# A convolution, spectral attention and FFN on one core: the main stage ordered by a table of places, 128-column weights in the last product, first pixels loaded ahead of the build

## The chip, the cores and the metric

One core of a Trainium2 chip runs the whole program in one launch. The metric is the device time of that launch in microseconds; each kernel is timed several times and the median counts. One further execution is recorded by the hardware profiler: all views of "the profile" and "the trace" come from it. PE is the matrix engine, PEld its weight loads, DVE, ACT and POOL are the vector, scalar and GpSimd engines, and SP only issues DMAs here.

## The reference, cut to what matters

The input x is 64 images of 55 x 55 pixels with 96 channels in float32. A depthwise convolution comes first, with a 25 x 25 kernel of which only every third row and column is non-zero and the centre is zero. Its result multiplies x. Then follow a spectral layer and a feed-forward layer, both residual and both on a layer norm over the channels, with each image taken as a sequence of 3025 tokens:

```python
x = conv(x, kernel * mask) * x + bias + x
t = x.reshape(64, 3025, 96)
h = relu(bn1(ln(t) @ w1.T))                      # 192 channels
X = fft(h, axis=1, norm='ortho')
xr = relu(X.real * rd - X.imag * idg + rb)
xi = relu(X.imag * rd + X.real * idg + ib)
t = t + bn2(ifft(xr + 1j * xi).real @ w2.T)
h = relu(qlinear(ln(t), W1, b1))                 # 384 channels, products in an 8-bit float
t = t + qlinear(h, W2, b2)
```

`qlinear` rounds its factors to a float with 5 exponent and 2 mantissa bits, and its sums to one with 10 mantissa bits (float16).

## The kernel before

**Build.** The convolution runs on PE with banded matrices made from the 81 taps. `sel` (selection matrices) and `kt` (taps) are loaded on SP's queue (L86 to L91), the network's constants on ACT's. For each of 56 PSUM banks, up to 20 small matmuls (L205) make a stretch of the bands; ACT copies the first 48 channels into `toep` (L214) and DVE the last 48 into `later` (L215), one 8.4 MB tile, which is then stored to DRAM as `tb` in six parts (L217). With that, the pools of the build are closed, and the output buffers of the convolution, `buf` (pool `c_ob`, six of them, L222), take their place in SBUF.

**Convolution.** The pixels of a third of the rows (r of 3), for half the images (bh of 2) and half the channels, form a group; there are 12. A group has four or three tiles of rows (`NTS`) and six steps of eight channels. `load` (L229) brings the x of a step, on SP's queue and always two steps ahead; the first two are asked for after `tb`'s stores (L304). `compute` (L237) takes two or three taps of tiles into a PSUM bank (L253), DVE adds 1 and multiplies by x into `buf` (L261), and POOL adds the bias (L271). `stores` (L275) gives the DMAs of a tile to the DRAM tensor `t1`, large ones on ACT's queue, small ones on POOL's. They are spread over the next group's steps, except that tiles whose buffer the next group needs at once are stored "early", right after their computing (L310 to L315). In the last group all three tiles are early, so their stores stand between the computing of one tile and the next. After the first six groups `toep` is refilled from `tb` (L317).

**Main stage.** Each of 64 sequences is a list of 289 tasks: load of t (L546), statistics (L560) and layer norm a (variance L508, root, reciprocal, Newton step L529), then seven times scale `xa`, turn `pa` (L587), copy `tnt`, and 13 times `ph` (L609), relu `h` (L618), transform `pf` (L624), copy `g` (L628), store to `gd`. Then come fetches `gt`; six spectral blocks (`px` L692, three ACT, four DVE and two POOL operations); four projections (`pd` L767, L777, `d` L786, `pe` L797, `e` L806); `ed` out and in; five inverse transforms `py` (L859) with residual and statistics; layer norm c; seven `xc`, `xq`, `pq` (L913), `tq`; nine times `pu` (L936), DVE's `y` (L945) and `z` (L948), ACT's `hq` (L960); five times `pw` (L981, "down": 15 matmuls, the weights of each being 121 columns of `hq`), ACT's and DVE's `o` (L990, L995), POOL's `ot` (L1001), store.

Every task has a place, a number in units of a sequence, which a formula gives, such as `at = fo + 0.231 + 1.552 * (...)[q]` at L1009. `ordered` (L371) goes through all tasks of all sequences with a model of each engine's time: for each engine, among the tasks that are free to run, it takes the one that can start soonest, but doesn't look past the first one that can start within 0.2 us by more than `NEAR` in place (0.359). The resulting order is written out as the program. Buffers (`bufs`, L464) come from pools with so many of each; PSUM has four small banks (`psn`) and two double ones (`psw`).

Of the kernel before, what the change touches and what calls it, by code (L numbers as in the profile page):

```python
# [11 lines left out]
F32 = mybir.dt.float32  # L12
# [29 lines left out]
NOB = 6  # L42
SU = 21
# [8 lines left out]

@with_exitstack
def conv_attn_hybrid(ctx, tc, a, out, t1, tb, gds, eds):
# [21 lines left out]
    with ExitStack() as cx:  # L76
# [9 lines left out]
        later = lp.tile([128, CHH, NE * TQ], F32, tag="later", name="later")  # L86
# [47 lines left out]
        for of in (toep, later):  # L134
            nc.gpsimd.memset(of[:, :, : 2 * TQ], 0.0)
            nc.gpsimd.memset(of[:, :, 16 * TQ :], 0.0)
# [61 lines left out]
        for j0 in range(0, TQ, 5):  # L198
            nj = min(5, TQ - j0)
            for e in range(2, 16):  # L200
# [14 lines left out]
                nc.vector.tensor_copy(later[:, :, cols], src[:, CHH:])  # L215
        for c0 in range(0, CHH, CC):
            nc.sync.dma_start(tb[:, c0 : c0 + CC], later[:, c0 : c0 + CC])  # L217
        first.close()

        ob = cx.enter_context(tc.tile_pool(name="c_ob", bufs=NOB))  # L222
        groups = [(0, r, bh) for r, bh in ((0, 0), (1, 0), (0, 1), (1, 1), (2, 0), (2, 1))]
        halfway = groups[-1]
        groups += [(1, r, bh) for bh in range(BH) for r in range(NR)]
        steps = [(n, c0) for n in range(len(groups)) for c0 in range(0, CHH, CC)]
        xts, bufs_ = {}, {}

        def load(n, c0):  # L229
            half, r, bh = groups[n]  # L230
            c1 = half * CHH + c0
            for m in range(NTS[r]):
                x = xp.tile([128, CC, NBS], F32, tag=f"x{m}", name=f"x{m}_{n}_{c0}")
                nc.sync.dma_start(x, a["xc"][bh, sum(NTS[:r]) + m][:, c1 : c1 + CC, :])
                xts[n, c0, m] = x
# [39 lines left out]
        def stores(n, m):  # L275

            half, r, bh = groups[n]
            rows_, buf, b0 = TPS[r], bufs_.pop((n, m)), bh * BB
# [3 lines left out]
            for i in range(nr):  # L282
                n0 = (3 * (rows_ * m + i) + r) * R
                large.append((
                    nc.sync if last and i % 2 else nc.scalar,
                    t1[b0 : b0 + BB, half, n0 : n0 + 48, :].rearrange("b (q s) c -> q b (s c)", s=3),
                    buf[at_row(i) : at_row(i) + 16].rearrange("q (b s) c -> q b (s c)", s=3),
                ))


            to = t1[b0 : b0 + BB, half].rearrange("b (y z) c -> y b (z c)", z=R)
# [12 lines left out]
        for step in steps[:2]:  # L304
            load(*step)
        for k, (n, c0) in enumerate(steps):
# [4 lines left out]
            for m in range(nt):  # L311
                compute(n, c0, m)
                if m < early:
# [6 lines left out]
            if ending:  # L320
                pending = [x for m in range(max(0, early), nt) for x in stores(n, m)]
# [21 lines left out]

    pools = {}
# [15 lines left out]
    tasks, users, edges = [], {}, {}  # L360
    FULL, SWITCH, NEAR, RING = "128x128", 0.09, 0.359, 8
    PLAIN = (FULL, FULL, 0.05, 0.05)

    def task(eng, cost, place, what, after=(), new=(), use=()):
        k = len(tasks)
        tasks.append((eng, cost, place, what, tuple(after), tuple(new), tuple(use) + tuple(h for h, _ in new)))
# [4 lines left out]
    def ordered(bufs):  # L371
# [11 lines left out]
        dma_free, last, landed = 0.0, PLAIN, []  # L383
# [22 lines left out]
        while len(order) < n:  # L406
            best = None
            for eng, q in queue.items():
# [3 lines left out]
                for place, k in q[:60]:  # L412
                    if first is not None and first[0] <= f + 0.2 and place > first[2] + NEAR:
                        break
                    r = max(f, ready_at[k])
                    wanted = [pool for _, pool in tasks[k][5]]
# [33 lines left out]
            else:  # L450
                free[eng] = end[k] = start + cost
            for h, pool in tasks[k][5]:
# [13 lines left out]
        e2=1, xc=2, xq=2, tq=1, hq=1, y16=2, z16=2, o16=2, ot=3, rstda=2, rstdc=2, mean=2, psn=4, psw=2,  # L466
# [4 lines left out]
    def make(h, pool, shape, dt=F32):  # L471
        k = count[pool] = count.get(pool, -1) + 1
        if pool == "tnt":
            live[h] = tnts[k % 2]
        elif pool in ("sm", "sr"):
# [23 lines left out]
    def layernorm_tasks(b, place, what, t, after, mean):  # L499

        st, rstd = (f"st{what}", b), (f"rstd{what}", b)
# [31 lines left out]

        new = [(mean, "mean")] if mean is not None else []
        k = task("POOL", 1.9 if new else 1.45, place + 0.048, variance, after, new=new, use=[st])
        k = task("ACT", 0.57, place, root, [k])
        k = task("DVE", 0.22, place, inverse, [k], new=[(rstd, f"rstd{what}")])
        return task("POOL", 1.12, place, newton, [k], use=[(rstd)])

    def sequence(b):  # L540
# [4 lines left out]
        def load():  # L545
            tt = make(t, "t", [NJ, 2, NR1, CHH])  # L546
            tv = t1[b].rearrange("h (j r) c -> j h r c", r=NR1)
# [3 lines left out]
        loaded = task("SP", (2, 0.41, 4.25), b - 0.85, load, new=[(t, "t")])  # L551
        sta = ("sta", b)
        ks = []
        for q in range(5):
# [9 lines left out]
            ks.append(task("DVE", 0.8, b - 0.6 - 0.214 + 0.06 * q, stats, after, new=new, use=[t] if new else [t, sta]))  # L564
        rstd = layernorm_tasks(b, b - 0.28, "a", t, ks, None)
        g_done = []
        for i in range(7):
            g0, ng = 4 * i, min(4, NR1 - 4 * i)
            at = b + 0.861 * (2 * i - 2.0) / 13
# [24 lines left out]
            k = task("POOL", 0.784 if ng == 4 else 0.31, at - 0.129, scale, [rstd], new=[(xa, "xa")], use=[t, ("rstda", b)])  # L594
            k = task("PE", 0.103 * ng, at, turn, [k], new=[(pt, "psn"), (tnt, "tnt")] + ([(gd, "gd")] if i == 0 else []), use=[xa])
            edges[k] = (FULL, FULL, 0.06, 0.1)
            turned_ = task("ACT", 0.1 + 0.087 * ng, at, turned, [k], use=[pt, tnt])
            ks = []
            for p in range(2 * i, min(2 * i + 2, 13)):
                nq = min(2, NR1 - 2 * p)  # L600
                at = b + 0.861 * p / 13
# [30 lines left out]
                k = task("PE", 0.326 * nq, at, hidden, [turned_], new=[(ph, "psn"), (h, "h")], use=[tnt])  # L632
                edges[k] = (FULL, FULL, 0.16, 0.16)
                k = task("ACT", 0.107 + 0.137 * nq, at, relu, [k], use=[ph, h])
# [510 lines left out]
```

## Time and profile before

| | us |
|---|---|
| median of 3 runs (lowest, highest) | 4614.85 (4613.04, 4620.83) |
| the profiled execution, and its span | 4654.67, 4652.9 |
| constants | 0 to 16 |
| build, PE busy throughout | 16.0 to 61.4 |
| PE idle: `tb` out, first x in | 62 to 86.5 |
| convolution, PE busy 789.5 of 863.9 | 86.5 to 950.4 |
| PE idle: handover | 950.4 to 1021.7 |
| main stage to the last `pf`, PE busy 3341.0 of 3496.3 | 1021.7 to 4518.0 |
| end, PE busy 102.4 of 134.9 | 4518.0 to 4652.9 |

The profiled execution is 0.9% longer than the median, and what is summed from its durations is compared with its own time first. Busy times of PE are modelled at their ends; where the pace of a row of matmuls matters, it is read from the starts in the timeline.

### The profile page before, as it was taken

To read this page: it belongs to the slowest core of one execution; us is meant where nothing else is said; L and a number is where in the kernel's file an instruction comes from. 1 tells how busy PE (TensorE), PEld (TensorE's weight loads), DVE (VectorE), ACT (ScalarE), POOL (GpSimd) and SP (SyncE) were. 2 spreads that over 40 slices of the span, in tenths; PEclk is the share of its full clock that TensorE was granted. 3 is DMA by queue.
4 is the path that set the end of the run, shared out by engine and by line. 5 is a ranking of instruction groups with operands and counts; after the bars stand their busy time and mean duration, and the time that the engine had idled before them with its cause. 6 is when DMAs were issued, how large, how long until landed. Compare 5 with 4: busy or idle time off the path is not lost.

```text
span 4652.9 us, 194788 instructions
## 1 busy us (share of the span) xinstructions
PE 4284.9 (92%) x83314; PEld 3569.2 (77%) x83314; DVE 3280.7 (71%) x7232; ACT 2963.2 (64%) x5947; POOL 3087.5 (66%) x4209
## 2 busy tenths in 40 slices
PE   7998798939999999999999999999999999999987
PEld 6998798937777777777777777777777777777775
DVE  4544354424888877877887788788787878788776
ACT  2000000017888888887887888888887888788875
POOL 1766576745666767766776666677766666677655
PEclk8999899969999999999999999999999999999996
DMA  4678888786666666766676666676666666667662
GB/s 162 166 193 204 245 197 207 190 185 165 165 171 178 179 177 178 181 177 169 180 183 169 169 174 179 172 185 180 176 183 169 177 174 176 171 179 183 177 162 71
DMA packets 572798, 823.14 MB, mean 177 GB/s; under 512 B 62127, under 2 KB 470276, under 8 KB 570268
## 3 DMA queue, kind: packets, MB, share of 16 engines
q1 hardware_dynamic: 442704, 736.10, 58.7%
q10 hardware_dynamic: 113036, 64.71, 7.1%
q0 software_dynamic: 16192, 9.86, 1.1%
q8 instruction: 655, 10.73, 1.0%
q14 instruction: 211, 1.73, 0.1%
HBM read 419.45 MB, written 390.64 MB: 174 GB/s over the span
## 4 chain that ended last, share of the span: by engine, by line
PE 71%; DVE 7%; DMA 7%; ACT 6%; issue 5%; POOL 2%; ACTq 2%; SPq 0%; POOLq 0%; DVEq 0%
PE pl L253 13%; PE pf L624 9%; PE ph L609 9%; PE pd L767 7%; PE px L692 7%; PE pw L981 5%; PE py L859 4%; PE pd L777 4%; PE pu L936 4%; PE pe L797 3%; PE pa L587 3%; DMA x<-in_xc_dram 2%; DMA t<-buf 2%; DVE y L945 2%; PE pq L913 2%
## 5 line engine op out<-in xcount | busy, mean ns | idle before, releaser
L253 PE MATMUL pl<-x,toep 128*64 128x96 f32 (+1 forms) x18432 | 790.1, 250 | 99.0 <-DVE buf L261 41.2
L253 PEld LDWEIGHTS pl<-x,toep 128*64 128x64 f32 (+1 forms) x18432 | 783.4, 137 | 105.7 <-issue 55.7
L945 DVE CAST y<-pu 128x1008 f16<-128x1008 f32 (+1 forms) x576 | 689.2, 1202 | 224.6 <-PE pu L936 220.5
L261 DVE SCALAR_TENSOR_TENSOR buf<-pl,x 121x384 f32<-121x384 f32 (+1 forms) x480 | 390.1, 842 | 499.0 <-PE pl L253 314.3
L609 PEld LDWEIGHTS ph<-w1e,tnt 97*121 97x121 f32 x3200 | 543.3, 185 | 210.9 <-issue 64.4
L960 ACT ACTIVATE hq<-z 128x1008 fp8e5<-128x1008 f16 (+1 forms) x576 | 601.2, 1050 | 156.7 <-DVE z L948 156.3
L718 DVE SCALAR_TENSOR_TENSOR m<-px,par,m 128x400 f32<-128x400 f32 x768 | 480.8, 626 | 286.3 <-ACT ar L709 201.6
L609 PE MATMUL ph<-w1e,tnt 97*121 97x192 f32 x3200 | 665.1, 330 | 12.9 <-ACT e L806 11.4
L271 POOL TENSOR_TENSOR buf<-buf,cbias 121x768 f32<-121x768 f32 (+1 forms) x240 | 434.1, 1821 | 363.9 <-DVE buf L261 252.1
L624 PE MATMUL pf<-h,f 121*128 121x384 f32 (+1 forms) x1664 | 664.8, 484 | 4.9 <-ACT h L618 2.6
L521 ACT ACTIVATE sm_s_a<-sm_v_a,eps 121x25 f32<-121x25 f32 x64 | 20.3, 318 | 959.0 <-POOL sm_v_a L512 956.6
L574 POOL TENSOR_TENSOR xa<-t,rstda 121x384 f32<-121x384 f32 (+1 forms) x448 | 348.2, 780 | 419.7 <-PE pa L587 411.7
L692 PE MATMUL px<-m,gt 50*64 50x50 f32 x24576 | 456.4, 220 | 63.1 <-issue 59.8
L692 PEld LDWEIGHTS px<-m,gt 50*64 50x64 f32 x24576 | 416.0, 136 | 122.0 <-issue 105.2
L725 POOL TENSOR_TENSOR sm<-ar,m 128x400 f32<-128x400 f32 x256 | 270.9, 1058 | 353.6 <-DVE m L718 296.4
L767 PE MATMUL pd<-w2e,sm 128*64 128x96 f32 x8192 | 415.7, 254 | 30.9 <-ACT g L628 18.0
L628 ACT COPY g<-pf 128x384 f32<-128x384 f32 (+1 forms) x832 | 385.6, 467 | 85.5 <-PE pf L624 70.6
L1001 POOL TENSOR_TENSOR ot<-t,o 121x480 f32<-121x480 f32 x320 | 374.3, 1177 | 91.2 <-DVE o L995 91.2
L618 ACT ACTIVATE h<-ph 121x384 f32<-121x384 f32 (+1 forms) x832 | 389.8, 488 | 68.3 <-PE ph L609 61.6
L948 DVE TENSOR_SCALAR z<-y,b1q 128x1008 f16<-128x1008 f16 (+1 forms) x576 | 418.9, 732 | 11.4
L767 PEld LDWEIGHTS pd<-w2e,sm 128*64 128x64 f32 x8192 | 358.6, 139 | 76.0 <-ACT g L628 22.5
L981 PEld LDWEIGHTS <-hq 128*121 128x121 fp8e5 x4800 | 315.9, 142 | 77.1 <-issue 37.6
(115 smaller groups left out, 8367.2 us busy)
## 6 DMA issues: line engine op xcount, KB each, us to landing
gd<-g SPq DMA_DIRECT2D x768, 192.0 KB
gt<-gd SPq DMA_DIRECT2D x512, 288.0 KB
x<-in_xc_dram SPq DMA_DIRECT2D x240, 384.0 KB
t<-t SPq DMA_DIRECT2D x64, 1050.0 KB
out_dram<-ot SPq DMA_DIRECT2D x320, 210.0 KB
t<-buf ACTq DMA_DIRECT2D x211, 288.0 KB
ed<-e SPq DMA_DIRECT2D x384, 150.0 KB
ed<-e SPq DMA_DIRECT2D x128, 131.2 KB
```

Source lines behind the costliest of these rows:

```text
L253: nc.tensor.matmul(pl[p : p + width, cc * NBS : (cc + 1) * NBS], toep[:, c0 + g + cc, o : o + width], xts[n, c0, m + d][:, g + cc, :], sta ...
L261: nc.vector.scalar_tensor_tensor(buf[:px, :, c0 + g : c0 + g + CG].rearrange("p n c -> p c n"), pl[:px, : CG * NBS].rearrange("p (c n) -> ...
L271: nc.gpsimd.tensor_tensor(part, part, cbias[:px, c1 : c1 + CC].unsqueeze(1).to_broadcast([px, NBS, CC]), ALU.add)
L609: nc.tensor.matmul(x[:NJ, q * H : (q + 1) * H], live[tnt][:, g * NJ : (g + 1) * NJ], w1e, start=True, stop=True,)
L624: nc.tensor.matmul(x[:, : nq * H], f1, live[h][:, : nq * H], start=True, stop=True)
L692: nc.tensor.matmul(x[to : to + 64].rearrange("p (q r n) -> p q r n", q=2, r=2)[:, k2p, :, o : o + NR1], y[rows, k % KC, c0 : c0 + 64], m1[ ...
L718: nc.vector.scalar_tensor_tensor(live[out_], view(px)[:, :, 256 : 256 + KC * NR1], scale, live[than], ALU.mult, ALU.max)
L767: nc.tensor.matmul(y[k % 2][64 * k2p : 64 * k2p + 64, k // 2 * CH : (k // 2 + 1) * CH], full[:, k, 64 * k2p : 64 * k2p + 64], w2e[:, 0, :] ...
L945: nc.vector.tensor_copy(live[y16][:, :n], live[pu][:, :n])
L948: nc.vector.tensor_scalar(make(z16, "z16", [128, 1024], F16)[:, :n], live[y16][:, :n], b1q[:, k : k + 1], 0.0, ALU.add, ALU.max,)
L960: nc.scalar.activation(live[hq][:, k, n0 : n0 + n], live[z16][:, :n], AF.Copy, saturate=False)
L981: nc.tensor.matmul(p[:NJ, g * CH : (g + 1) * CH], live[hq][:, k, n0 : n0 + NJ], w2q[:, k, :], start=(k == 0), stop=(k == 2),)
```

## The change

1. *Places.* A table of 289 numbers, one for each task of a sequence in the order in which they are defined, replaces the formulas: task k of the program gets `k // 289 + PLACES[k % 289]`. `NEAR` goes from 0.359 to 0.5.
2. *The model in `ordered`.* DVE's two bias tasks (`z`, L948, and `o`, L995) are put into `alone`: in the model they don't run at the same time as anything on POOL. A pool `small` of two stands for the small tiles of the layer norms. The cost given to `down` is 0.66 instead of 0.84, that to the bias of `o` 0.33 instead of 0.6.
3. *down.* `hq` becomes one fixed tile `hidden8` with seven zero columns at its end, in the pool `late`, and each weight of `pw` has 128 columns (of which the last seven give PSUM rows that nothing reads).
4. *Start.* The x of the first two steps are loaded first of all on SP's queue. The order of the groups' (r, bh) in the first half changes, so that the first group has three tiles. `later` becomes three tiles of 16 channels, with three copies for each bank.
5. *Handover.* In the last group the stores follow all the computing. `t1` becomes two DRAM tiles, one for each half of the images. The loads of sequences 0 and 1 are one DMA each, on POOL's queue.

```diff
+CPL = 16
+PLACES = (
+    -2.368, -0.491, -1.741, -2.267, -1.88, -4.257, -1.46, -0.301, -1.857, -0.171, -0.314, -0.137, -0.467,
...
+)
-        later = lp.tile([128, CHH, NE * TQ], F32, tag="later", name="later")
+        later = [lp.tile([128, CPL, NE * TQ], F32, tag=f"later{k}", name=f"later{k}") for k in range(CHH // CPL)]
+        groups = [(0, r, bh) for r, bh in ((1, 0), (0, 0), (1, 1), (0, 1), (2, 0), (2, 1))]
...
+        for step in steps[:2]:
+            load(*step)
         kt = selp.tile([128, CH], F32, tag="kt", name="kt")
         nc.sync.dma_start(kt, a["taps"])
...
                 nc.scalar.copy(toep[:, :, cols], src[:, :CHH])
-                nc.vector.tensor_copy(later[:, :, cols], src[:, CHH:])
+                for k, of in enumerate(later):
+                    c1 = CHH + CPL * k
+                    nc.vector.tensor_copy(of[:, :, cols], src[:, c1 : c1 + CPL])
         for c0 in range(0, CHH, CC):
-            nc.sync.dma_start(tb[:, c0 : c0 + CC], later[:, c0 : c0 + CC])
+            k, c1 = c0 // CPL, c0 % CPL
+            nc.sync.dma_start(tb[:, c0 : c0 + CC], later[k][:, c1 : c1 + CC])
...
-        groups = [(0, r, bh) for r, bh in ((0, 0), (1, 0), (0, 1), (1, 1), (2, 0), (2, 1))]
...
-                if m < early:
+                if m < early and n + 1 < len(groups):
...
-                pending = [x for m in range(max(0, early), nt) for x in stores(n, m)]
+                pending = [x for m in range(nt) if (n, m) in bufs_ for x in stores(n, m)]
...
+    hidden8 = late.tile([128, 3, NJ * NR1 + 7], F8, tag="hidden8", name="hidden8")
+    nc.gpsimd.memset(hidden8[:, :, NJ * NR1 :], 0.0)
...
-    FULL, SWITCH, NEAR, RING = "128x128", 0.09, 0.359, 8
+    FULL, SWITCH, NEAR, RING = "128x128", 0.09, 0.5, 8
...
-    def task(eng, cost, place, what, after=(), new=(), use=()):
+    def task(eng, cost, what, after=(), new=(), use=()):
         k = len(tasks)
+        place = k // len(PLACES) + PLACES[k % len(PLACES)]
...
                     r = max(f, ready_at[k])
+                    if eng == "POOL":
+                        r = max(r, shared)
+                    elif k in alone:
+                        r = max(r, free["POOL"])
...
                 free[eng] = end[k] = start + cost
+                if k in alone:
+                    shared = end[k]
...
-            tv = t1[b].rearrange("h (j r) c -> j h r c", r=NR1)
+            tv = t1s[b // BB][b % BB].rearrange("h (j r) c -> j h r c", r=NR1)
+            if b < 2:
+
+                nc.gpsimd.dma_start(tt, tv)
+                return
             for p0, p1 in split(NJ):
                 nc.sync.dma_start(tt[p0:p1], tv[p0:p1])
...
-                            p[:NJ, g * CH : (g + 1) * CH],
-                            live[hq][:, k, n0 : n0 + NJ],
+                            p[:, g * CH : (g + 1) * CH],
+                            live[hq][:, k, n0 : n0 + 128],
                             w2q[:, k, :],
...
-            k = task("PE", 0.84, at, down, [hq_done[s, k] for s in range((1, 2, 2, 3, 3)[q]) for k in range(3)], new=[(pw, "psn"), (o16, "o16")], use=[hq])
+            k = task("PE", 0.66, down, [hq_done[s, k] for s in range((1, 2, 2, 3, 3)[q]) for k in range(3)], new=[(pw, "psn"), (o16, "o16")], use=[hq])
```

In the program that results, the same tasks are issued on every engine, in another order.

## The prediction

> **What bounds the kernel now.** I read the page's head and 40 slices first, then the chain of waits at both ends of the convolution, then a table of windows, and last PE's waits and timeline in the steady part.
>
> From the page, its totals and PE's slices:
> ```profile
> span 4652.9 us, 194788 instructions
> PE 4284.9 (92%) x83314; PEld 3569.2 (77%) x83314; DVE 3280.7 (71%) x7232; ACT 2963.2 (64%) x5947; POOL 3087.5 (66%) x4209
> ...
> PE   7998798939999999999999999999999999999987
> q8 instruction: 655, 10.73, 1.0%
> ```
> PE is the bound wherever its digit is 9. It is less in the first slice, inside the convolution (slices 4 to 7), at the handover (the single 3, slice 9) and at the end. Windows (from:to and length; busy PE, PEld, DVE, ACT, POOL; granted clock, DMA share, GB/s) of two such places and of the steady main stage:
> ```profile
> 62.00:86.50 24.50, 0.58 (x4) 0.30 (x4) 0.11 (x1) 0.00 (x0) 0.00 (x0) 0.59 0.97 387
> 1400.00:4400.00 3000.00, 2873.43 (x53815) 2290.36 (x53813) 2411.38 (x5611) 2475.43 (x4968) 2102.78 (x3132) 0.99 0.68 177
> ```
> In the steady 3000 us, 2700 matmuls of ph at 50 a sequence make 54 sequences: 55.55 us each, of which PE is idle 2.34. All else in that stage is PE's own pace, and ACT at 82.5% comes next. The chain at the start and at the handover, in time order (start, length, piece):
> ```profile
> 16.02 45.35 PE pt L205 x1064
> ...
> 69.18 17.25 DMA x<-in_xc_dram
> ...
> 977.76 12.12 DMA t<-buf
> 989.96 13.86 DMA t<-t
> ...
> 1009.45 10.08 issue
> ...
> 1021.70 1.85 PE pa L587 x8
> ```
> After the build PE is idle 25 us while the stores of tb fill the DMA engines (0.97) and the first pixels land behind them. At the handover it is idle from 950.4 to 1021.7: last stores, first load of t, statistics, and 10.08 us in which sequence 0's reciprocal stands on DVE behind the statistics of sequence 1. In the steady part PE's waits (engine and line, releaser, total, times, longest) lead with:
> ```profile
> PE px L692 <- issue: 48.4, 50, 2.3
> PE pd L767 <- ACT g L628: 16.6, 27, 0.8
> ...
> PE ph L609 <- ACT e L806: 10.6, 27, 0.4
> ```
> About 82 of the 126.6 idle us are "issue", the rest waits for engines. The "issue" holes sit in long runs of small matmuls (px, pd, pe): two on the timeline, 2553.88 and 2558.45, are 4.57 us and 256 instructions (128 matmuls, 128 weight loads) apart; queue q8's 10.73 MB in 655 packets are 16.4 KB each. So I read them as PE reaching the next 256 instructions before they have been fetched.
>
> **What the Trainium skill says.** "TensorE: Matmul & The Clock Gate", section "Weight-path perf modes — Fast Weight Load (FWL) and DoubleRow": a weight load is fast, about twofold, when the number of weights is 128 and the type isn't FP32. The trace agrees; loads of min/median/max ns:
> ```profile
> L936 PEld LDWEIGHTS <-w1q x1152: 95/98/181, 1145.6 to 4637.1; 96*128 96x128 fp8e5 x192
> L981 PEld LDWEIGHTS <-hq x4800: 129/137/230, 1157.7 to 4646.3; 128*121 128x121 fp8e5 x192
> ```
> "SBUF — State Buffer", section "Who interferes with whom": a DVE operation in a two-port mode, or one with two SBUF inputs against a GpSimd read, takes the shared port alone and the other stands. L948 (372/597/1405 ns) and L995 (343/550/1308) spread as that says. "DMA: Bandwidth & Descriptors", section "Why a DMA increments its semaphore by 16 and not by 1": a transfer is dealt to the largest number of engines up to 16 that divides its rows, so 121 rows would get 11; no trace here shows it.
>
> **The change, part by part,** against the profiled run (4654.67, span 4652.9); the median shown, 4614.85, is 0.9% lower, so I scale at the end.
>
> *Start.* The first two steps' x (6 x 393 KB) now go ahead of kt and sel on SP's queue: 2.36 MB, about 6 us at the 387 GB/s above. The build starts at 16.02 behind the constants' chain (sc, w1e, pm), not behind sel, so this hides; sel's last part would land near 17. Three copies per bank on DVE instead of one (240 elements, by the trace's 240-element copies near 0.38 us each) stay below the 0.81 us that PE takes per bank (45.35/56). Then the convolution's matmuls can begin near 62.5, but DVE's first eviction writes buf, which lies over `later`, and so waits for all six stores of tb, until about 85. Eight PSUM banks hold only 4 of 2 taps at 1.32 us and 2 of 3 taps at 1.98, then 2 at 1.32 more: 11.9 us of PE work. So the gain is 12, not the 24 that the gap suggests. The other group order makes one more early store and costs nothing that I see.
>
> *Handover.* The last group's stores now follow all its computing, so POOL's last bias additions are no longer behind store issues: a few us earlier. t1 in two tiles frees nothing new: by region the loads of the first 32 sequences never waited for the other half's stores. Against the gain, hidden8 moves the pool of t upward until it reaches over the conv buffers, and the first loads of t_0 and t_2 now wait for the last stores on every DMA lane; then t_0 and t_1 (one DMA each on POOL's queue, of 121 rows), t_2 to t_4 (SP) and m1, m2 (ACT) all start together. Behind the waiting loads stand, on POOL, only work that needs t_0, and on SP t_3 and t_4, which aren't used for 100 us. The reciprocal is still queued on DVE behind t_1's statistics. I get 69 to 75 us against 71.3: 0, with 8 to 10 either way.
>
> *down with 128 columns.* On the timeline 15 matmuls of pw take 0.83 us (2576.16 to 2576.99), 55 ns each. Here 96 rows move (the 7 new columns are cleared once, on an idle POOL); pq moves 121 in 54 ns, so 96 should take 43 to 44. With loads of the 98 ns kind hidden, 15 x 44 = 0.66. 320 x 0.17 = **-54 us** of PE. Bounds: 0 (if pw's pace isn't the load's) and -60. Idle cover isn't in question: PE is the bound.
>
> *The order.* What the two programs issue on PE can be counted. Changes between full-array and 64-wide tiles: 716 before, 950 after. A ph followed by px lasts 0.74 us on the timeline instead of 0.65, so 0.09 each: 234 x 0.09 = +21. Short tasks (pa, pq, pw) directly ahead of ph or pf: 258 before, 384 after, at 0.01 (after pa) to 0.06 (after pq): +5, up to 8. PE's work is thus -54 + 21 + 5 = **-28**.
>
> *Fetch.* Runs of at least 128 small matmuls fall from 62 to 2, yet the densest 8 us hold as many instructions (640), and the densest 12 us hold 892 instead of 764. With one block of 256 instructions every 4.0 us and one block in hand, before's order loses 108 us over the main stage, near the 82 x 64/54 = 97 of the trace; after's loses 139 by the same sum. Bounds 0 and +31, I take **+15**: breaking the long runs should help more than my simple sum allows.
>
> *Engine waits.* 40 us in 54 sequences are 47 in 64, with start and end about 58. Slack, in PE work placed between producer and consumer, moves both ways: sm to pd at the 10th percentile 18.0 to 23.3 us, sr to pd2 11.3 to 18.1, hq to pw 2.3 to 4.6; but ph to pf has a median of 2.74 before and 1.30 after (10th percentile 1.72 and 0.81), pa to ph 2.87 and 1.30. A relu takes 0.49 (L618, mean 488 ns), and with both handoffs some 0.75 must fit. The waits on g and e (16.6 and 10.6) are for PSUM or buffers that ACT frees late; DVE is eased since z and o no longer run beside POOL (to near their minima, about 4 us a sequence). I take **-20**, between -58 and a growth that is priced as a rival.
>
> *End.* After the last pf, PE's pace of what is left is 67.4 us before and 61.7 after (its share of down included, already counted); 132 us pass in the trace, so most of the end is waiting on chains, which a shorter list improves a little: **-8**, 0 to -20.
>
> Sum: -12 + 0 - 28 + 15 - 20 - 8 = -53. 4614.85 x (1 - 53/4654.67) = **4562**.
>
> **The rivals.**
> *R1, a larger gain.* DVE's relief lets nearly all engine waits go (-58 for -20) and fetch holes stay as they are (0 for +15): -53 - 38 - 15 = -106, so 4510. For it: longer slack at every join of the spectral part. Against: ph to pf at half its former distance.
> *R2, slower.* One mechanism: ph to pf is placed at half its former distance, and ACT, at 82.5%, is late by more than the slack. The place is pf L624 <- ACT h, over 832 pf. It decides from 53/832 = 0.064 us per pf, where it undoes the forecast; I price it at 0.11, +92 less 53 = +39: **4653**. For it: a 10th percentile of 0.81 against 0.75 needed. Against: in the trace pf waited for h only 2.0 us in 54 sequences, and PE's queue delays itself, so one late relu makes the next one early.
> *R3, fetch takes it.* The densest stretches stall by the full +31, waits unchanged and the switches at 0.11 (+5), no gain at the end: -12 - 28 + 31 + 5 = -4, so 4611, no change to be told.
> *R4, the ends don't change as said.* The early pixels only move the wait to x of the third step or to the evictions (0 for -12), and the loads of t wait for the last stores (+10): -31, so 4584.
>
> **How the numbers follow.** Forecast 0.50, R1 0.15, R2 0.15, R3 0.10, R4 0.10. The likeliest is 4562, its own range 4535 to 4590 (waits, fetch and handover at half their bounds). For 8 in 10 the range takes in R1 (to 4505), R3 and R4, and cuts into R2: 4505 to 4640. A measurement of this kernel tells 0.2% (9 us) from no change: faster is the forecast, R1, R4 and a little of R3, 0.77; same 0.07; slower 0.16.
>
> **What would show it.** Loads of L981 near 98 ns and 15 pw in 0.66 to 0.67; PE idle from about 75 to 86 instead of 62 to 86; a gap at the handover of 62 to 80; L948 and L995 with medians near 400 and 360; PE busy in a steady 54 sequences lower by 20 to 30 us; px and pd "issue" near 90 to 115 us. Wrong if pf waits on h for over 50 us (R2), if "issue" doubles, or if pw keeps its 0.83.

## The result and the profile after

The changed kernel takes 4843.51 us (median of 4, 4833.11 to 4855.8) against 4617.84 for the kernel before, a ratio of 1.0489 (95% interval 1.0458 to 1.052). The prediction had 4562 and a range that ended at 4640. The profiled execution of the changed kernel took 4833.11 us.

| stage, us from the span's start | before | after |
|---|---|---|
| first matmul of the convolution | 85.6 | 60.3 |
| last matmul of the convolution | 950.4 | 919.0 |
| first `pa` of the main stage | 1021.7 | 1008.5 |
| main stage up to the last `pf`, length | 3496.7 | 3687.4 |
| end, length | 134.5 | 135.4 |

All of the loss, 190.7 us in these two profiles, lies in the main stage (in a second profile of each kernel it is 259.8 us, from 3484.9 to 3744.7). The two ends of the convolution together gave 13 us, which is what the sum had for them, though by other parts. From the page of the changed kernel, its head, PE's slices and the granted clock:

```profile
span 4831.3 us, 194630 instructions
PE 4327.9 (90%) x83314; PEld 3517.7 (73%) x83314; DVE 3215.5 (67%) x7344; ACT 2987.3 (62%) x5947; POOL 3085.4 (64%) x4216
...
PE   8999898569899998998999999999999999999996
...
PEclk9999999879999999999999999999999999999996
```

PE does the same 83,314 matmuls, those of `down` faster than before, and yet is busy 43 us longer. In the steady window (busy PE, PEld, DVE, ACT, POOL; clock, DMA share, GB/s):

```profile
1400.00:4400.00 3000.00, 2762.03 (x50927) 2135.55 (x50926) 2221.67 (x5310) 2362.10 (x4702) 1984.03 (x2961) 0.97 0.64 167
```

That is 51.2 sequences instead of 54.0, with every engine less busy than before, DMA too, and a clock of 0.97 instead of 0.99. No engine became the bound: time fell into holes. PE's waits in that window say which:

```profile
PE px L739 <- issue: 50.4, 51, 3.0
PE pe L844 <- issue: 36.4, 20, 3.9
PE pd L824 <- issue: 33.2, 21, 4.0
PE py L905 <- DMA e<-ed: 27.1, 19, 3.1
PE px L739 <- DVE y L988: 22.7, 26, 0.9
PE pw L1024 <- issue: 14.2, 9, 2.9
PE pq L956 <- POOL xq L947: 10.2, 19, 0.7
```

`pe` and the second half of `pd` (L844, L824) now stand in "issue" holes of up to 4 us. In the kernel before, px alone had more than half of that time (48.4 of 84.5 us), and 2.6 us was the longest:

```profile
PE pd L777 <- issue: 12.4, 10, 2.6
PE pe L797 <- issue: 6.6, 8, 1.5
```

Two waits are new: `py` for ed's fetch, and px for a double bank of PSUM that DVE's `y` frees late. What a long hole costs besides itself is seen on PE's timeline (start, length, what, count, idle time before and its releaser) and in three windows around one:

```profile
2287.32 0.55 PE L824 MATMUL pd<-w2e,sr 64*64 64x96 f32 x13
2291.87 1.06 PE L824 MATMUL pd<-w2e,sr 64*64 64x96 f32 x18 [4.00 <-issue]
...
2298.16 3.28 PE L905 MATMUL py<-e,i 128*121 128x480 f32 x4
```
```profile
2280.00:2290.00 10.00, 7.52 (x252) 6.72 (x252) 9.26 (x36) 6.42 (x15) 3.15 (x10) 1.00 0.83 239
2291.00:2301.00 10.00, 9.13 (x91) 6.07 (x92) 1.04 (x2) 4.32 (x9) 4.79 (x6) 0.50 0.25 64
2302.00:2312.00 10.00, 10.00 (x53) 7.28 (x52) 9.57 (x35) 6.53 (x15) 4.95 (x11) 1.00 0.85 177
```

After a hole of 4.00 us the clock is granted at 0.50 for the next 10 us, and four `py` take 3.28 us instead of 4 x 0.41. PE counts as busy all that time. That is where much of its additional busy time comes from.

Counted over the steady window, in us for one sequence (pace: from one matmul's start to the next, less idle time; the clock's part is what PE's tasks in windows at 0.5 took above the same tasks' pace at 1.0):

```
                        period  issue holes  waits for data  slow clock  pace at full clock
before                   55.56     1.56          0.73           0.57          52.69
after                    58.59     2.97          1.58           1.23          52.81
```

Two further counts in the trace settle what these holes are. Of the "issue" holes over 0.2 us (86 before, mean 0.98 us; 115 after, mean 1.32 us), every one stands at instruction 193 or 194 of PE's records modulo 256, and the matmul that ends it starts a median of 2.5 to 2.6 us after the start of a 16,384-byte packet on the instruction queue q8. So a hole is the border of a block of 256 instructions that has arrived late. And of the windows of half clock (17 before, 30 after), every one begins about where a hole over 1.2 us ends, "issue" or data (from 0.9 us before that end to 1.7 us after it).

Why a block is late can be read from the same packets, one of which brings the next block while PE runs the present one. In the table, the blocks that PE runs in under 4.5 us (its holes not counted) are sorted by the share of the DMA engines' time that data packets take in the first 2.5 us of the block. Given are the blocks, the median time from the block's start to the start of the next block's packet, and the holes at the next block's border:

| DMA share | before | after |
|---|---|---|
| under 0.8 | 72 blocks, 1.1 us, holes 23.2 us | 94 blocks, 1.2 us, holes 15.8 us |
| 0.8 to 0.9 | 34 blocks, 1.7 us, holes 14.8 us | 27 blocks, 1.4 us, holes 21.5 us |
| 0.9 and more | 43 blocks, 1.6 us, holes 36.7 us | 70 blocks, 2.3 us, holes 94.7 us |

In the blocks that PE takes longer over, the packet starts later in the same way: after 1.1 us under 0.8 and after 2.7 (before) and 2.6 us (after) at 0.9 and more. So late packets go with busy DMA engines whether PE runs densely or not, and density decides whether PE has to wait for them. The new order makes more dense blocks (191 instead of 149) and lets more of them meet busy DMA engines: 34 of its 55 "issue" holes over 1.2 us begin within 6.5 us of the issue of a fetch `gt`, where before it was 6 of 29. This is read from the traces; no run took the data away at these places.

At the start, the same profile shows 12 us of early work and then the wait for DVE's first eviction, as forecast:

```profile
60.30 11.39 PE L287 MATMUL pl<-x,toep 128*64 128x96 f32 x272
72.51 0.88 PE L287 MATMUL pl<-x,toep 128*64 128x96 f32 x16 [0.82 <-issue]
85.66 14.52 PE L287 MATMUL pl<-x,toep 128*64 128x96 f32 x304 [12.28 <-DVE buf L295]
```

At the handover, the chain of waits (start, length, piece) shows, behind the last store, the load of m and then a load of t. That load takes 23.79 us, where before it took 13.86:

```profile
944.55 15.30 DMA t<-buf
...
960.85 7.22 DMA m<-in_m_dram
968.09 23.79 DMA t<-t
...
991.95 4.10 DVE sta L611 x25
...
997.51 8.83 issue
```

### The profile page after: what moved, and what is told of

The parts are those of the page before. It is cut to its first block, busy times and chain, and to the rows that moved or that the text cites. A ratio compares the mean times of both kernels' runs of the same rounds, so it can differ in the third digit from the quotient of the medians.

```text
span 4831.3 us, 194630 instructions
## 1 busy us (share of the span) xinstructions
PE 4327.9 (90%) x83314; PEld 3517.7 (73%) x83314; DVE 3215.5 (67%) x7344; ACT 2987.3 (62%) x5947; POOL 3085.4 (64%) x4216
## 4 chain that ended last, share of the span: by engine, by line
PE 63%; DMA 14%; ACT 7%; issue 6%; DVE 4%; POOL 3%; ACTq 2%; SPq 1%; POOLq 0%; DVEq 0%
PE pl L287 12%; PE pf L673 9%; PE ph L658 8%; PE py L905 6%; PE px L739 5%; PE pd L814 5%; PE pe L844 4%; DMA e<-ed 4%; PE pu L979 3%; DMA gt<-gd 3%; PE pw L1024 3%; PE pd L824 3%; PE pa L637 3%; DMA x<-in_xc_dram 2%; DMA t<-buf 2%
## 5 line engine op out<-in xcount | busy, mean ns | idle before, releaser
L658 PE MATMUL ph<-w1e,tnt 97*121 97x192 f32 x3200 | 654.3, 332 | 3.2 <-issue 1.8
L1003 ACT ACTIVATE hidden<-z 128x1008 fp8e5<-128x1008 f16 (+1 forms) x576 | 598.4, 1045 | 29.0 <-DVE z L991 26.3
L658 PEld LDWEIGHTS ph<-w1e,tnt 97*121 97x121 f32 x3200 | 529.1, 185 | 115.8 <-issue 19.7
L624 POOL TENSOR_TENSOR xa<-t,rstda 121x384 f32<-121x384 f32 (+1 forms) x448 | 335.7, 758 | 395.3 <-PE pa L637 375.0
L739 PE MATMUL px<-m,gt 50*64 50x50 f32 x24576 | 470.4, 221 | 99.0 <-issue 61.6
L1044 POOL TENSOR_TENSOR ot<-t,o 121x480 f32<-121x480 f32 x320 | 364.1, 1146 | 229.4 <-DVE o L1038 223.3
L673 PEld LDWEIGHTS pf<-h,f 121*128 121x128 f32 x1664 | 293.0, 195 | 166.0 <-ACT h L667 68.4
L947 POOL TENSOR_TENSOR xq<-xc,rstdc 121x384 fp8e5<-121x384 f32 (+1 forms) x448 | 350.0, 784 | 69.7 <-PE pq L956 53.6
L765 DVE SCALAR_TENSOR_TENSOR d<-px,par,nc 128x400 f32<-128x400 f32 x384 | 241.4, 629 | 198.0 <-ACT nc L756 106.3
```

What stands on the lines that cost most here:

```text
L658: nc.tensor.matmul(x[:NJ, q * H : (q + 1) * H], live[tnt][:, g * NJ : (g + 1) * NJ], w1e, start=True, stop=True,)
L673: nc.tensor.matmul(x[:, : nq * H], f1, live[h][:, : nq * H], start=True, stop=True)
L739: nc.tensor.matmul(x[to : to + 64].rearrange("p (q r n) -> p q r n", q=2, r=2)[:, k2p, :, o : o + NR1], y[rows, k % KC, c0 : c0 + 64], m1[ ...
L765: nc.vector.scalar_tensor_tensor(live[out_], view(px)[:, :, 256 : 256 + KC * NR1], scale, live[than], ALU.mult, ALU.max)
L1003: nc.scalar.activation(live[hq][:, k, n0 : n0 + n], live[z16][:, :n], AF.Copy, saturate=False)
```

## The experiments

**Which part of the change.** Four kernels on one chip. `old_order` is the changed kernel with the main stage's order as it was (formulas, settings of `ordered`); the start, the handover and `down` stay changed.

```diff
-        place = k // len(PLACES) + PLACES[k % len(PLACES)]
...
-    FULL, SWITCH, NEAR, RING = "128x128", 0.09, 0.5, 8
+    FULL, SWITCH, NEAR, RING = "128x128", 0.09, 0.359, 8
```

> The changed kernel with the old order of the main stage (formulas, NEAR 0.359, no exclusive ports, old costs); the start, the handover and the 128-column weights stay changed. Theory O (the order is at fault: dense stretches on PE outrun the fetch of instructions, and each hole is followed by a slower granted clock): main stage 3497 less 54 = 3440 us from the first pa to the last pf, total about 4550, 'issue' on PE about 1.5 to 1.7 us a sequence, slow clock about 1.3 to 1.6 us a sequence. Theory D (the faster weights are at fault, since they raise the pace of instructions): main stage stays above 3600, total above 4700.

Measured: 0.9977 (0.995 to 1.0004), with a main stage of 3505 us in a profile near the upper end of its times. So the order carries the loss: 5 points stand between this kernel and the changed one. But 0.9977 is not the 0.986 of theory O either; `down` and the ends bring less than their sum.

`new_order_121` takes only the 128-column weights back:

```diff
-                            live[hq][:, k, n0 : n0 + 128],
+                            live[hq][:, k, n0 : n0 + NJ],
```

> The changed kernel with weights of 121 columns in down. Theory O: still slower than before, 4850 to 4900, since PE gets 54 us more work of which the holes hide a part. Theory D: near 4620 or faster, 'issue' back to 1.5 us a sequence.

Measured: 1.054 (1.0507 to 1.0573). Theory D falls: without the faster weights the kernel is no faster. Its ratio is half a point higher, which is about the width of the intervals.

`old_places` keeps all settings of the changed planner and puts the values of the old formulas into its table.

> The changed kernel with the old formulas' values in its table of places; NEAR 0.5, the exclusive ports and the new costs in the planner stay. Theory O1 (the table makes the order bad): total 4550 to 4620, 'issue' near 1.6 us a sequence. Theory O2 (the planner's settings make it bad, whatever the table): total 4750 or more, 'issue' and the waits for y and ed as in the changed kernel.

Measured: 1.0387 (1.0355 to 1.0419), with a slow clock of 4.15 us a sequence, more than in the changed kernel. O1 falls: the old places under the new settings lose 4.1 points against `old_order`, nearly as much as the new table.

`old_order_pool` is `old_order` with hidden8 where hq stood:

```diff
-    hidden8 = late.tile([128, 3, NJ * NR1 + 7], F8, tag="hidden8", name="hidden8")
+    hidden8 = []
...
+            if not hidden8:
+                hidden8.append(sb("hq", [128, 3, NJ * NR1 + 7], "hidden8", F8, 1))
```

> As old_order, but hidden8 is taken from the place in SBUF that hq had, so that the pool of t stays below the convolution's buffers. Theory H (the loads of t wait for the last stores because t overlaps those buffers): PE's gap at the handover falls from about 89 to 72 us or less, total 15 to 20 us below old_order. Rival: the gap is set by the transfers that share the DMA engines, and changes by less than 5 us.

Measured: 0.9865 (0.9828 to 0.9901), and 0.9888 (0.9856 to 0.9919) once more on another chip. This version beats both kernels. PE's gap at the handover is 54.1 us against 85.7 in `old_order`, more than theory H asked for; of the some 50 us by which the total fell, that is 31. The loads of sequences 0 and 1 on POOL's queue are issued 22 us earlier. Their issue in `old_order`, then in `old_order_pool`, where DVE's statistics of sequence 0 follow (start, length, what, count, idle time before):

```profile
968.24 1.60 POOL L563 DMA_DIRECT2D t<-t  x2 [17.79 <-DMA m<-in_m_dram]
```
```profile
946.48 1.61 POOL L565 DMA_DIRECT2D t<-t  x2
964.07 6.48 DVE L579 BATCH_NORM_STATS2 sta<-t 121x6 f32<-121x96 f32 x40 [44.38 <-DMA t<-t]
```

The last store of `old_order_pool` lands only at 968.7, when these statistics are already running. So the first loads no longer wait for it.

> old_order_pool once more on this chip: ratio to before 0.985 to 0.99, faster than before for certain.

**Are the holes the loss?** Two kernels in which PE has fewer instructions at nearly equal work, with tasks and order untouched: in each px the upper half of the partitions comes from two wide matmuls, which don't give the transform there.

```diff
+                            if to:
+                                if k == hh:
+                                    nc.tensor.matmul(
+                                        at[:, :, : KC * NR1].rearrange("p r (k n) -> p r k n", n=NR1),
+                                        y[rows, k % KC, c0 : c0 + 64],
+                                        m1[rows, kk - k : kk - k + KC, :].rearrange("p k (r n) -> p r k n", r=2),
...
+                                continue
```

> The changed kernel, in whose px (L739) the 16 matmuls that fill the upper half of PSUM's partitions (of the 32 of a px) become two of 400 moving columns with one weight each, so that this half of the transform isn't computed as it should be; all tasks and their order stay. PE has about 330 of its 2600 instructions of a sequence less to fetch, all of them in the densest stretches, at about the same work. Theory F (holes from the fetch of instructions, and the slow clock after them, are most of what the new order costs): 'issue' falls from 2.97 to 1.2 us a sequence or less, slow clock from 2.99 to 2.0 or less, total by 100 to 180 us. Rival W (the new order's waits for data, ed, y and xq, and PE's own pace are most of it): 'issue' is replaced by other waits, total by less than 60 us.

> The same thinner px in old_order_pool. Theory F: 'issue' falls from about 1.9 to 0.8 us a sequence or less, total by 50 to 90 us, so that the new order's disadvantage, 6.3% between the changed kernel and old_order_pool, shrinks to 2 to 4% between the two thin kernels. Rival W: the disadvantage stays above 5%.

Measured: the new order goes from 1.0489 to 1.0074 (1.0057 to 1.0092), the old one from 0.9865 to 0.968 (0.9649 to 0.9711). PE's waits in the new order, thin:

```profile
PE py L917 <- DMA e<-ed: 54.6, 37, 3.0
PE px L751 <- DVE y L1000: 23.6, 27, 0.9
PE pq L968 <- POOL xq L959: 15.8, 26, 0.6
PE px L751 <- issue: 10.8, 14, 1.6
```

"issue" over all lines falls from 2.97 to 0.52 us a sequence, slow clock's windows from 2.99 to 0.83 us, PE's pace in px changes little (6.8 to 6.7 us a sequence). The new order wins 4 points, the old one about 2. So the holes and the clock after them were some 2 of the 5 points by which the orders differ. The other 3 stay, and part of the gain is taken by `py`, whose wait for ed doubles: W isn't the whole, but it isn't nothing. Between the two thin kernels a sequence differs by 1.83 us (56.26 and 54.43). Of these, 1.12 us are waits for data and 0.19 us "issue"; the rest is slow clock and PE's pace.

**Which setting of the planner.** `near_05`, `true_costs` and `alone_only` are `old_order_pool` with one setting changed each.

```diff
-    FULL, SWITCH, NEAR, RING = "128x128", 0.09, 0.359, 8
+    FULL, SWITCH, NEAR, RING = "128x128", 0.09, 0.5, 8
```

> old_order_pool with NEAR 0.5 in the planner instead of 0.359, nothing else. Theory O2 (any order that the planner makes anew lacks what the old one had by its fit to the chip): 2 to 5% slower than old_order_pool. Theory O3 (the exclusive ports or the costs are at fault, not NEAR): within 1% of old_order_pool.

> old_order_pool with the planner's cost of down 0.66 instead of 0.84 and of the bias of o 0.33 instead of 0.6, nothing else. Theory O2: 2 to 5% slower than old_order_pool. Theory O3 with the exclusive ports at fault: within 1% of old_order_pool; with the costs at fault: over 2% slower.

> old_order_pool with the exclusive ports in the planner's model and nothing else (NEAR 0.359, old costs, old places). Theory O2 (any new planning loses): 3 to 6% slower than old_order_pool. Theory O3 (only NEAR and the costs harm, the ports are a truer model): within 1% of it.

Measured: 1.0462 (1.0423 to 1.0502), 1.05 (1.0451 to 1.0549), 1.0547 (1.051 to 1.0584), each 6 to 7 points above `old_order_pool`. O3 falls for all three, and the loss is larger than O2 expected. It isn't longer holes of the fetch: "issue" is 2.0 to 2.2 us a sequence here, against 1.6 and 2.0 in the two profiles of `old_order_pool`, while the waits for data are 3.4 to 3.8 us against 0.9 to 1.0. These waits are spread over many pairs, and differ from order to order; common to all is the clock, at 0.5 for 4.4 to 5.2 us a sequence against 0.8 to 1.1. The pool `small` wasn't tried alone.

**The parts of the sum alone.** `down_only` and `start_only` are the kernel before with one part of the change; `before_again` is the kernel before, for the spread between profiles.

> The kernel before with 128-column weights in down and nothing else (hidden8 at the place of hq, the order unchanged). If PE's work decides: 0.98 us of pw less in each sequence is 63 us, ratio 0.987. Theory F (part of it goes back as holes in the fetch, since the same instructions are asked for in less time): 15 to 35 us, ratio 0.992 to 0.997, 'issue' above that of the kernel before.

Measured: 0.9951 (0.9936 to 0.9967), some 23 us. The loads are fast (L990 in this kernel), and `pw` falls by 0.98 us a sequence:

```profile
L990 PEld LDWEIGHTS <-hidden x4800: 94/98/153, 1159.3 to 4615.4; 128*128 128x128 fp8e5 x192
```

But the reason that I expected for the rest is wrong: "issue" stays at 1.56 us. In its place stand some 0.2 us a sequence by which the other tasks got slower (pq most, 68 to 72 ns a matmul), and waits that were absent or about half as long at most in the kernel before:

```profile
PE pa L596 <- ACT o L999: 5.8, 11, 0.7
PE pq L922 <- POOL xq L913: 4.5, 16, 0.3
...
PE ph L618 <- ACT d L795: 3.0, 15, 0.2
PE pf L633 <- ACT o L999: 2.8, 9, 0.3
```

I read the lines of `o` as PE coming to the next task earlier and finding the bank that ACT's `o` empties not yet free.

> The kernel before with the start of the changed one and nothing else (first pixels ahead of the build, later in three tiles, order of the first half's groups). My sum: the convolution ends 12 us earlier, ratio 0.997. Rival: it ends 30 us earlier, as in the changed kernel's profile against that of before, ratio 0.993 to 0.995.

Measured: 0.9941 (0.9924 to 0.9959), 27 us. The gap at the start is 12.2 us here, so 12 us come from there. Another 11.3 us are a wait in the old order of groups that the sum had passed over. In the kernel before it stands at 454.7 on PE's timeline, and on DVE's its cause, a buffer whose stores aren't done:

```profile
466.01 4.71 PE L253 MATMUL pl<-x,toep 128*64 128x96 f32 x72 [11.29 <-DVE buf L261]
```
```profile
465.15 3.45 DVE L261 SCALAR_TENSOR_TENSOR buf<-pl,x 121x384 f32<-121x384 f32 x5 [18.71 <-DMA t<-buf]
```

With the new order of groups no hole near this place is over 3.5 us. The order of groups wasn't tried without the early pixels.

> The kernel before once more, to see how far one profile of it stands from another: 'issue' between 1.4 and 2.3 us a sequence, main stage 3460 to 3510 us, end of the convolution 935 to 955.

Measured: 4634.11 us; main stage 3484.9, end of the convolution 946.2, "issue" 1.50, slow clock's windows 0.94 us a sequence (1.33 in the first profile).

**Can the waits for data be taken out?** `new_order_py_later` moves the tasks py in the finished order:

```diff
-        for k in ordered(bufs):
+        for k in postponed(ordered(bufs), 3):
```

> The changed kernel, in whose order each inverse transform py goes three PE tasks later where the buffers allow it (some 224 of 320), with what needs it after it. If the wait of py for ed is a loss of its own: it falls from 0.53 to under 0.2 us a sequence and the total by 20 to 40 us. Rival: the idle time turns up at the next late task (pq on xq, px on y), and the total moves by less than 12 us.

Measured: 1.0596 (1.0554 to 1.0638), slower by a point, so neither forecast of the total came. The wait for ed is still there (0.69 us a sequence), and a new one has come, of pf for `h`, now that other tasks stand before py:

```profile
PE pf L703 <- ACT h L697: 38.5, 89, 0.7
PE py L935 <- DMA e<-ed: 34.4, 20, 3.6
```

`new_order_fetch_early` leaves PE alone and issues ed's fetch sooner on SP's queue:

```diff
-        for k in ordered(bufs):
+        for k in sooner(ordered(bufs)):
```

> The changed kernel; on SP's queue alone, each fetch of ed (L895) is issued right after the last store of its ed (L884) instead of behind one to three tasks of other sequences. Theory Q (the wait of py for ed comes from SP's queue: 7.4 us from that store to the fetch, against 3.7 in the kernel before): the wait falls from 0.53 to 0.1 us a sequence or less, and the total by 25 to 60 us with the slow clock that followed it. Rival: SP, which now waits there for the store to land, is late with the others' transfers, other waits take the place, and the total moves by less than 15 us.

> The changed kernel with hidden8 at the place in SBUF that hq had, the order unchanged. Theory H: PE's gap at the handover falls from 89 to about 55 us as it did with the old order, total by 30 to 38 us (ratio to before near 1.041). Rival: with the new order the gap is set by the statistics on DVE, and falls by less than 15 us.

Measured, both on one chip: 1.0396 (1.0355 to 1.0437) and 1.0316 (1.028 to 1.0352). In `new_order_fetch_early` nothing stands on SP between the last store of ed and the fetch, yet the fetch is still issued 7.4 us after it: SP's order behind the stores wasn't what held it. What stands ahead of the stores may be. In the changed kernel a load of t is issued right before them on SP's queue, in all 51 sequences of the steady window (start, length, what, count):

```profile
2566.21 0.74 SPq L600 DMA_DIRECT2D t<-t  x2
2567.05 2.08 SPq L884 DMA_DIRECT2D ed<-e  x4
...
2576.61 0.71 SPq L895 DMA_DIRECT2D e<-ed  x1
```

That load is 1134 KB, and the DMA engines are busy to 0.94 in the 3.5 us after the last store. In the kernel before, the load of t comes at least 4 us earlier in every sequence, the share is 0.46, and the fetch follows after 3.8 us. `new_order_fetch_early` leaves the load where it was; a kernel that moves it wasn't tried. The wait for ed is 0.32 us in both kernels, with and without the edit (0.53 and 0.71 in two profiles of the changed kernel), so theory Q has no support in the traces. For `new_order_pool`, the gap at the handover is 58.0 us, 31 below the changed kernel's 89.5: theory H holds with the new order too. Between the two kernels stand 0.8 points, about 37 us, and 28 of them are the gap (86.3 in the first). Both ratios lie about a point lower than the traces account for. That chips differ by so much for this order would explain it, but this isn't shown.

`new_order_less_out` leaves out most stores of the output; `after_again` ran beside it.

> The changed kernel without the large stores of out for q of 1 to 4 (L1050), so that four fifths of the 105 first rows of the output aren't written; some 50 MB of 823 less on the DMA engines, in SP's queue. Theory M (the data transfers delay PE's fetch and the stores of ed): 'issue' falls below 2.5 us a sequence and the wait for ed below 0.2, total by 40 us or more. Rival: the fetch is late by PE's own density alone: 'issue' stays within 0.3 of 2.97, total by less than 15 us.

> The changed kernel once more, on the same chip as the next two, so that the loss of the new order is measured against old_order_pool without the difference between chips: ratio to before 1.035 to 1.05; 34 us of it are the handover.

Measured: 1.0441 (1.0385 to 1.0498) and 1.0505 (1.0456 to 1.0554). PE's waits without those stores:

```profile
PE px L739 <- issue: 48.5, 51, 2.6
PE pd L824 <- issue: 45.2, 24, 4.3
PE pe L844 <- issue: 37.0, 21, 3.6
PE px L739 <- DVE y L988: 22.8, 26, 0.9
PE py L905 <- DMA e<-ed: 16.8, 13, 2.8
```

"issue" is 3.15 us a sequence against 3.22 in `after_again`, with 13 GB/s less on the DMA engines (152 against 165). The total is 0.6 points lower, some 30 us, with intervals that overlap: it lies between theory and rival. Theory M isn't refuted by this. The stores that were left out didn't lie where the holes are: 67 dense blocks still meet DMA engines that are busy to 0.9 and more (69 in `after_again`), and their holes are 105 us (91). For ed's wait (0.33 against 0.71) M may hold, but 0.32 was also seen with all stores.

## Why the prediction was wrong

The two profiles each of `old_order_pool` and of the changed kernel give what the order costs for one sequence: period 55.25 to 58.95, of it "issue" 1.76 to 3.10, waits for data 0.94 to 1.63, slow clock 0.40 to 1.36, PE's pace at full clock 52.13 to 52.86. That is 3.7 us, and 238 in 64 sequences. Against the forecast's -53 the medians show +226. The terms below are off by 71 us (fetch), 64 (waits), 61 (clock), 31 (down), 21 (switches) and 8 (end), together 256 of the 279 us between the two. By the terms of the sum:

- *Start, -12.* The gap's 12 us were right, by the mechanism named (eight banks, DVE's first eviction behind `tb`'s stores). The order of groups, which "costs nothing that I see", probably gained the 15 more (11.3 of them seen as the wait that went). `start_only`: -27.
- *Handover, 0.* The overlap of t with the convolution's buffers was seen, its price not: the loads of t wait for the last store, go out together with m's and take 23.8 us. It costs 31 us (`old_order` to `old_order_pool`, `new_order_pool`), so that the gap went from 71.3 to 89.5 instead of to some 55. The other edits of the handover gave the 12 to 17 us from 66.6 and 71.3 (two profiles of before) to 54.1; which of them did isn't shown. Its error and that of the start cancel, so that the right sum of the two ends was luck.
- *down, -54.* Loads (98 ns instead of 137, which is 1.4-fold and not about twofold) and pace (15 in 0.64 us) came as forecast, but the term assumed that "PE is the bound" makes every us of PE count. `down_only` gave 23: the next tasks and ACT's `o` took back the rest.
- *The order's switches, +26.* The pace at full clock rose by 0.73 us a sequence, 47 us. Right in kind, too small. Counted at the changes between full-array and 64-wide tiles themselves (11.0 and 14.5 a sequence in one pair of profiles) it is 0.47 us, 30 us; the rest lies inside runs of one task.
- *Fetch, +15.* This is the step that failed. Measured: 1.34 us a sequence, 86 us, beyond the upper bound of 31. The mechanism, late blocks of 256 instructions, was named, and the position of every hole in its block bears it out. But I let one count (fewer long runs of small matmuls) outweigh the other that stood beside it, 892 instead of 764 instructions in the densest 12 us. `pw` and `pq` between px and pd are little relief: 15 matmuls of `pw` are 30 instructions in 0.64 us, four of ph 8 in 0.65. And "one block every 4.0 us" was the spacing inside one dense run, taken as fixed. A block is late by when its packet starts (1.1 us after the start of the block before it, or 2.3 with busy DMA engines) and by 2.5 us more to its first matmul. Which transfers run during the dense runs was no part of the sum. (The "about 82" us of "issue" in the prediction are 84.5 with pq's.)
- *Nothing for the clock.* The sum had no such term, and gave no reason for that. A hole over 1.2 us may bring 3.4 to 10.2 us at half clock, 0.96 us more a sequence, 61 us. The kernel before had it too (its 0.99), in holes of 1.3 us and more after which tasks take twice their time; the timeline would have shown it.
- *Engine waits, -20.* They rose by 0.69 us a sequence, 44 us: ed, `y` and xq came, g, e and `o` went. I judged slack by the tenth percentile of a few pairs; the pairs that became late (ed's fetch to py, `y` to px) weren't among them. DVE was eased as forecast (z's median 597 to 481 ns, `o`'s 550 to 400), and nothing in these sums shows what it bought.
- *End, -8.* It was 0 (134.5 and 135.4).

Of the rivals, R3 named the mechanism, too small and without the clock. R2 named ACT's `h`: `pf` waits for it only 3.1 us in the steady window, so the slower side came at another place. R4's view of the loads of t was right, its view of the first pixels wrong. One sign misled: px and pd were to stand in "issue" for 90 to 115 us, and did for 91.6. But pe and pw, which that sign left out, went from 11.3 to 50.6 us.

Shown is: the order is the loss; the holes are late blocks of instructions; they and the clock are about 2 of its 5 points. Read from the traces, but tested by no run, is that the blocks come late where the order lets dense runs meet busy DMA engines. Of the remaining 3 points, the larger part is waits for data in the profiles of the two thin kernels. Not settled is what causes each of these waits, and why every order that the planner made with another setting loses 4 to 7 points, all four with hardly more "issue" than the old order had. That the old formulas and settings had been fitted to each other on the chip would account for it; only the loss is shown.

## What to carry to other kernels

A stream of many small matmuls is bounded by instructions as well as by work: count instructions in windows of the order, all tasks together, before trusting a better plan, and see which transfers run at the same time. Price a hole on PE with what follows it, since beyond 1.2 us it cost half of the next 3 to 10 us in about half of the cases here. An engine that is busy 96% of the time returned only part of what its work is shortened by (here 23 of 63 us), and an order that a planner makes is not better for a truer model: measure it.

## What was not expected of the hardware

- The Trainium skill, "TensorE: Matmul & The Clock Gate", section "HAM oscillation — how this bites in real kernels", puts the rule at no idle gaps over about 3.4 us. Here gaps from 1.27 us upward stood in front of slow windows: of 29 holes over 1.2 us in the kernel before 17 were followed by one, of 68 in the changed kernel 30, among them all 8 of 3 us and more. That windows last 3.4 us or a multiple, and that PE runs at half, agrees (`py` 800 ns against 408).
- PE's instructions come in blocks of 256, one packet of 16,384 bytes on q8 each (655 in a run), and every "issue" hole over 0.2 us of the steady window stands at the same place of a block.
- Where a buffer lies in SBUF moved the handover by 31 us: 9,096 bytes ahead of a pool pushed it over buffers that were still being stored.
